# Layer 0 of a two-layer model on one core: the second batch's attention placed within the Sinkhorn chain, branch sums on GpSimd, and the mix taken from PSUM copies in two halves

## The chip, the core and the metric

The kernel runs on one core of a Trainium2 chip. The core has a matrix engine (TensorE, in profiles PE; its weight loads are PEld), a vector engine (VectorE, DVE), an activation engine (ScalarE, ACT), a general engine (GpSimd, POOL) and a queue engine (SyncE, SP) that issues DMAs. Each works through its own instructions in order and waits on semaphores for the others. SBUF is the working memory, PSUM the memory that matmuls write to; GpSimd does not use PSUM here.

The metric is the device time of one execution, in microseconds (us). Several runs are made, and their median is given. A profile is one further execution, with its own time and its own span.

## The reference

Two batches of 1024 rows, 512 wide, go through two layers. Layer 0, cut to what matters here:

```python
xn = _layernorm(x)
x = x + _L0_attn_ref(xn, ...) + _L0_ffn_ref(xn, ...)
# attention: one head of 128
out = softmax(q @ k.T * scale) @ v ;  out @ Wo + bo
# ffn: four streams of 128 columns
H_res = sinkhorn_log((x_norm @ W_res.T).reshape(B, T, 4, 4) + H_res_base)   # 50 iterations
H_pre, H_post = softmax(x_norm @ W_pre.T + ...), softmax(x_norm @ W_post.T + ...)
H_res = (1 - g) * I + g * H_res
y = einsum('btnc,btn->btc', x_streams, H_pre) @ W_branch
x_mixed = einsum('btij,btjc->btic', H_res, x_streams)
return x_mixed + einsum('btc,btn->btnc', y, H_post)
...
def step(carry, _):
    u = -logsumexp(Z + v[..., None, :], axis=-1)
    v = -logsumexp(Z + u[..., :, None], axis=-2)
```

Layer 1 has causal attention with 32 heads in 8 groups over low-rank keys and values, and beside it a linear layer with routed low-rank parts. It needs the normed output of layer 0, first through its "latents", a projection of all 1024 rows of a batch.

## The kernel before

Rows lie in tiles of 128, eight to a batch; `acc[b, t]` is the running sum of tile t of batch b, an SBUF tile of 128 x 512. Matmuls take float16 pairs (a high and a low part, three products), so most data is split: ACT writes the high part, DVE or POOL subtracts it for the low part. `normed_T` normalises a tile, splits it and has SP transpose it by DMA. Its `pool` argument says which engines do that.

The kernel is written against a framework that schedules when the program is complete: an instruction earlier in the program has the higher priority, a simulated timeline decides when its inputs and buffers are there, and the result is a fixed order on every engine. Buffers come from pools by tag ("P" three, "PT" three, "xr" four, "f2k" four, "wo" five, "wq" four, "h2k" three; in PSUM "s" four, "pp" three, "av" one). `tc.issue_after(i)`, and `after(...)` around it, put the instructions of a block behind instruction i on its engine.

The order of layer 0 in the program (lines 897 to 948):

- `front0(0)`: norm, transposes, values and ffn logits, Q and K of batch 0.
- `sinkhorn(0)` is a generator. It begins on line 471, and its iterations for batch 0 are in `chain_dve` (line 542), in linear form: `Kt`, the exponentials of the 4 x 4 matrices of 1024 rows (128 x 128 numbers), lies in PSUM; each iteration multiplies, sums and takes the reciprocal over rows (lines 551 to 553), then over columns (556 to 558), all on DVE, each instruction needing the one before. The column sum reads `M` with its last two axes exchanged. At iteration 25 the sums are taken back into the logarithms (560 to 564). There are 100 yields; `adv(n)` moves the chain by n of them. At the end lines 508 and 510 write `Hm`, from which the mix is computed.
- Batch 0's attention in two halves of four row blocks. A row block is a `row_step`: scores on PE, two evictions with a row minimum on DVE (`rows_exp`, L272), exponential on ACT (L276), scaling into the high part (L295, or L292 and L293), the low part on DVE (L301) or, where `LP[b]` names the block, on POOL (L299), and a DMA transpose (L303). `attn0_out` then multiplies by the values (L328), projects (L465, L467) and adds to `acc` on DVE (L469). Between these calls the chain is advanced by `CA = 5` steps per row block.
- `branch0(0)`: y = the branch, scaled on ACT (L420), summed on POOL. `CB = 1` step per tile.
- `front0(1)` and `branch0(1)`, with `CC = 2` steps at each of 16 places and `CB` at eight.
- `adv(200)`: the rest of the chain. `hm0` is its last instruction.
- The weights of layer 1's first group (`load_q`, `kv0`) on POOL's queue.
- Two groups of four tiles (`LG`): `mix0_units`, then `layernorm_tiles`, then `xT_tile` for each. A unit loads x again and norms it on ACT (L579), then works five streams: four of x, the fifth of y. For the tiles in `MP` ACT multiplies into a tile `m` (L592) and POOL adds it to `acc` (L593); for the others DVE does 4 fused multiply-adds a stream (L602), the first from `acc` into a PSUM tile `d`, the last back into `acc`.
- `layer1_attn` calls `start`: the latents of batch 0 from the first four tiles, four q units, the latents of the other four, keys and values of group 0, and then `attn0_1()`: batch 1's attention of layer 0, whose row blocks stand behind `hm0`.

After that come 16 groups of layer 1 (eight heads groups for each batch) with 32 row blocks each. Further work is put at numbered steps by `put`: the chain of batch 1 (on POOL), its mix, `branch0_add(1, t)` (the branch's product and addition, lines 434 and 436), gating, and the ffn blocks; those of batch 1 at every second step from the start of the last group.

Of the kernel before, what the change touches and what calls it, by code (L numbers as in the profile page):

```python
# [16 lines left out]
P = 128  # L17
# [13 lines left out]
NR = P // QR  # L31
LG = ((0, 1, 2, 3), (4, 5, 6, 7))
MP = (1, 3, 6, 7)
NP = (2, 2, 2, 2, 0, 2, 0, 2)
LP = ((0, 1, 2, 4, 5, 6, 7), (0,))
F0 = (((0, 1, 2, 3), (4, 5, 6, 7)), (range(0, 8),))
FP = ((0, 2, 0, 2, 0, 2, 0, 2), (2, 2, 2, 2, 2, 2, 2, 2))
X1 = 7
CA, CB, CC = 5, 1, 2
SK0, SKN, MX0, MXN, LN1 = 1, 116, 122, 74, 198  # L40

G0, G1, GL, WT, LX, LA = 16, 200, 3, 220, 231, 240
# [9 lines left out]
def tile_model(ctx: ExitStack, tc: tile.TileContext, out: bass.AP, a: dict):  # L52
# [126 lines left out]


    last_pool, last_row, last_T = [None], [None], [None]
    last_hi, last_lo, last_hm = [None], [None], [None]

    def after(*insts):

# [21 lines left out]
    def layernorm_tiles(b, mv, rs, ts):  # L207
        ve = T("ve", [P, NT], bufs=2)
        sl = slice(ts[0], ts[-1] + 1)
        for t in ts:  # L210
            st = T("bnst", [P, 6], bufs=2)
            V.bn_stats(st, acc[b, t])
            V.bn_aggr(mv[:, t, :], st)
        V.tensor_scalar(ve[:, sl], mv[:, sl, 1], LN_EPS, None, ALU.add)
        rsqrt(rs[:, 0, sl], ve[:, sl], "rs")
        V.tensor_scalar(rs[:, 2, sl], rs[:, 0, sl], 4.0, None, ALU.mult)
        V.scalar_tensor_tensor(rs[:, 1, sl], mv[:, sl, 0], -1.0, rs[:, 2, sl],
                               ALU.mult, ALU.mult)

    def normed_T(b, mv, rs, t, dst, pool, tags=(("f2k", FB), ("h2k", HB))):  # L220

        xn = T(tags[0][0], [P, NC, P], bufs=tags[0][1])
        xf = xn.rearrange("p c d -> p (c d)")
        hl = T(tags[1][0], [P, NC, 2, P], F16, bufs=tags[1][1])
        if pool == 2:
            A.activation(xf, acc[b, t], AF.Identity, scale=rs[:, 2, t:t + 1], bias=rs[:, 1, t:t + 1])
        elif pool:
            G.tensor_scalar(xf, acc[b, t], rs[:, 2, t:t + 1], rs[:, 1, t:t + 1], ALU.mult, ALU.add)
        else:
            V.tensor_scalar(xf, acc[b, t], rs[:, 2, t:t + 1], rs[:, 1, t:t + 1], ALU.mult, ALU.add)  # L230
        last_hi[0] = A.activation(hl[:, :, 0, :], xn, AF.Copy)
        eng = G if pool else V
        lo = eng.tensor_tensor(hl[:, :, 1, :], xn, hl[:, :, 0, :], ALU.subtract)
        (last_pool if pool else last_lo)[0] = lo
        last_T[0] = nc.sync.dma_start_transpose(dst, hl.rearrange("p c l d -> p (c l d)"))

    def proj_T(w, xT, half):
# [7 lines left out]
    def srow():  # L245
        count[0] += 1
        return ps.tile([P, 512], F32, tag="s", name=f"s_{count[0]}", bufs=BS)
# [223 lines left out]
    def sinkhorn(b, lg):  # L471
# [33 lines left out]

        chain = chain_dve if b == 0 else chain_pool
        yield from chain(b, Z, M, aa, bb, over_i, over_j, f2)
        V.tensor_scalar(Hb, M, gs[:, 0:1], None, ALU.mult)
        for n in range(4):
            last_hm[0] = V.tensor_scalar(Hb[:, :, n, n], Hb[:, :, n, n], gs[:, 1:2], None, ALU.add)  # L510

    def chain_pool(b, Z, M, aa, bb, over_i, over_j, f2):

# [27 lines left out]

    def chain_dve(b, Z, M, aa, bb, over_i, over_j, f2):

        cols = M.rearrange("p t i j -> p t j i")
        Kt = srow()[:, :NT * 16].rearrange("p (t i j) -> p t i j", i=4, j=4)
        A.activation(Kt, Z, AF.Exp)
        x = Kt
        yield
        for it in range(1, 50):
            if x is not Kt:  # L550
                V.tensor_tensor(M, Kt, over_i(bb), ALU.mult)
            V.tensor_reduce(aa, x, AX.X, ALU.add)
            V.reciprocal(aa, aa)
            x = M
            yield
            V.tensor_tensor(f2(M), f2(Kt), over_j(aa), ALU.mult)  # L556
            V.tensor_reduce(bb, cols, AX.X, ALU.add)
            V.reciprocal(bb, bb)
            if it == 25:
                A.activation(aa, aa, AF.Ln)  # L560
                A.activation(bb, bb, AF.Ln)
                V.tensor_tensor(f2(Z), f2(Z), over_j(aa), ALU.add)
                V.tensor_tensor(Z, Z, over_i(bb), ALU.add)
                A.activation(Kt, Z, AF.Exp)
                x = Kt
            yield
        V.tensor_tensor(M, M, over_i(bb), ALU.mult)

    def mix0_units(b, t, rs, pool, y=None, hh=None):


        got = {}

        def load():
            xr = got["xr"] = T("xr", [P, H], bufs=XB)
            with after(t0):
                nc.sync.dma_start(xr, a["x"][(b * NT + t) * P:(b * NT + t + 1) * P, :])
            if b == 0:
                A.activation(xr, xr, AF.Identity, scale=rs[:, 2, t:t + 1], bias=rs[:, 1, t:t + 1])  # L579
                return  # L580
            with tc.issue_after(p0.ins):
                G.tensor_scalar(xr, xr, rs[:, 2, t:t + 1], rs[:, 1, t:t + 1], ALU.mult, ALU.add)

        n = NC if y is None else NC + 1

        def stream(j):
            xj = y if j == NC else got["xr"][:, j * P:(j + 1) * P]
            by = [hh[:, t, 1, i:i + 1] if j == NC else Hm[b][:, t, i, j:j + 1] for i in range(NC)]
            if pool:
                m = T("f2k", [P, H], bufs=FB)  # L590
                for i in range(NC):
# [1 line left out]
                G.tensor_tensor(acc[b, t], acc[b, t], m, ALU.add)  # L593
                return

            if j == 0:
                got["d"] = PP()
            for i in range(NC):
                sl = slice(i * P, (i + 1) * P)
                src = acc[b, t] if j == 0 else got["d"]  # L600
                dst = acc[b, t] if j == n - 1 else got["d"]
                V.scalar_tensor_tensor(dst[:, sl], xj, by[i], src[:, sl], ALU.mult, ALU.add)  # L602

        return [load] + [lambda j=j: stream(j) for j in range(n)]

# [302 lines left out]
    attn0_out(0, 0, f0[0][2], PTs)  # L910
    PTs = attn0_rows(0, 1, *f0[0][:2], lambda: adv(CA))
    attn0_out(0, 1, f0[0][2], PTs)
    f0[1] = front0(1, lambda: adv(CC))
    y4s = branch0(1, *f0[1][3:5], lambda: adv(CB))
    adv(200)
    hm0 = last_hm[0]

    def attn0_1():
        for half in range(2):
            with after(hm0):  # L920
                PT = attn0_rows(1, half, *f0[1][:2])
            attn0_out(1, half, f0[1][2], PT)

    def new_xT(b):
        xT1[b] = T("xT", [P, NT, 2 * NC, P], F16, bufs=1)

    def xT_tile(b, t, pool):
        normed_T(b, *ln1[b], t, xT1[b][:, t], pool)

    def tile_of(b, t):  # L930
        d = T("h2k", [P, 2 * NC, P], F16, bufs=HB)
        normed_T(b, *ln1[b], t, d, True, (("f2k", FB), ("xr", XB)))
        return d

    for hh in range(4):
        load_q(0, hh)
    kv0 = kv(0, 0)
    kv0[1][0]()
    new_xT(0)
    ln1[0] = layernorm(0, "b")  # L940
    for k, ts in enumerate(LG):
        units = [mix0_units(0, t, f0[0][5], t in MP, ys0[t], f0[0][4]) for t in ts]
        for fs in itertools.zip_longest(*units):
            for f in fs:
                f()
        layernorm_tiles(0, *ln1[0], ts)
        for t in ts:
            xT_tile(0, t, NP[t])

    def start(kvf, q):  # L950
        latents(0)
# [5 lines left out]
            lat_evac(0, mc, 1, lat_block(0, wl[:, mc], 1))  # L957
        for f in kvf:
            f()
        attn0_1()  # L960

    gw1 = gating_w()
    chain = sinkhorn(1, logit[1])
# [58 lines left out]
    put(58, 2, ffn_w)  # L1022
    for t in range(NT):
        put(0, FF + t, lambda t=t: ffn_block(0, t))
        put(60, 2 * t, lambda t=t: ffn_block(1, t))
    layer1_attn(kv0, start, extra)


# [45 lines left out]
```

## Time and profile before

| what | value |
|---|---|
| median of 3 runs | 1951.74 us (1942.79 to 1952.55) |
| the profiled execution's own time | 1957.52 us |
| its span | 1955.7 us, 35314 instructions |
| busy, PE / DVE / ACT / POOL | 1746.8 / 1506.1 / 1201.5 / 885.5 us |
| chain's first exponential (L546) | 48.19 us |
| `Hm` complete (L592 begins) | 183.03 us |
| first matmul of the latents | 235.3 us |
| first score of layer 1 (128 x 32) | 279.1 us |
| PE busy in 1100 to 1900 us | 98 to 100 of each 100 us |

The span is the time between the first and last event of the profile; the execution's time is a little longer. A row of the windows names a stretch and gives for each engine the busy microseconds and the number of instructions. A group's row names line, engine, operation, the tile written and the tiles read, the shape, and how many there were. A wait's row says which instruction waited for which, and for how long in total. Idle time of an engine that is not on the path costs nothing.

### The profile page before, as it was taken

The numbers are of one execution on the slowest core, as the hardware profiler recorded it, in microseconds if no ns is written. First come the engines' busy times: TensorE is split into PE (matmuls) and PEld (weight loads), VectorE is DVE, ScalarE is ACT, GpSimd is POOL, SyncE is SP. The second block draws the span as 40 slices with busy tenths as digits, with TensorE's granted clock in tenths as the row PEclk, the third lists the DMA queues.
The fourth block names the chain that finished last, engine by engine and source line by source line (L and its number), as shares of the span: only waits on it lengthen the run. The fifth ranks groups of instructions, "written<-read, shape, count | busy, mean of one in ns | idle before, by whom it ended". The sixth has DMA issues, their size and how long they took to land. (4 is left out here: it accounts for less than half of the span.)

```text
span 1955.7 us, 35314 instructions
## 1 busy us (share of the span) xinstructions
PE 1746.8 (89%) x11458; PEld 1051.5 (54%) x11458; DVE 1506.1 (77%) x4065; ACT 1201.5 (61%) x2924; POOL 885.5 (45%) x1527
## 2 busy tenths in 40 slices
PE   4771499989998999989889899999999999999997
PEld 3340245555564555555554556666566666656654
DVE  8889768988786878787875676777778787878665
ACT  4752864566665777776544565767666666666554
POOL 5553429676766655444631636060515152436010
PEclk9885699999999999999989999999999999999999
DMA  6430524565654656465753864655555565657446
GB/s 200 87 65 10 126 58 98 126 126 113 124 120 95 136 112 143 107 127 117 156 120 52 166 131 119 130 122 133 123 129 128 128 131 119 134 117 156 94 93 138
DMA packets 707308, 230.27 MB, mean 118 GB/s; under 512 B 689953, under 2 KB 690081, under 8 KB 707122
## 3 DMA queue, kind: packets, MB, share of 16 engines
q1 hardware_dynamic: 691666, 180.75, 45.7%
q0 software_dynamic: 13152, 43.07, 8.4%
q10 hardware_dynamic: 2304, 4.20, 0.7%
q8 instruction: 90, 1.47, 0.3%
q14 instruction: 96, 0.79, 0.1%
HBM read 52.81 MB, written 4.19 MB: 29 GB/s over the span
## 5 line engine op out<-in xcount | busy, mean ns | idle before, releaser
L301 DVE SCALAR_TENSOR_TENSOR Phl<-P,r,Phl 128x1024 f16<-128x1024 f32 (+31 forms) x520 | 483.2, 935 | 179.3 <-ACT Phl L295 168.5
L276 ACT ACTIVATE P<-P,nm 128x1024 f32<-128x1024 f32 (+31 forms) x528 | 391.9, 742 | 315.7 <-DVE nm L268 301.2
L88 PE MATMUL s<-K,Q 128*128 128x512 f16 (+22 forms) x2400 | 450.7, 320 | 88.9 <-DVE sk L556 38.2
L328 PE MATMUL av<-PT,V 128*128 128x256 f16 x3648 | 458.8, 277 | 27.8 <-DMA PT<-Phl 18.2
L295 ACT ACTIVATE Phl<-P,r 128x1024 f16<-128x1024 f32 (+31 forms) x520 | 379.8, 737 | 115.2 <-DMA PT<-Phl 95.0
L328 PEld LDWEIGHTS <-V 128*128 128x128 f16 x3648 | 360.0, 99 | 127.8 <-DMA PT<-Phl 22.2
L88 PE MATMUL pp<-wo,ao 128*128 128x512 f16 x1536 | 373.8, 380 | 18.1 <-ACT ao L103 17.0
L285 POOL MEMSET Phl<- 128x192 f16 (+2 forms) x384 | 77.3, 204 | 655.9 <-DMA PT<-Phl 525.4
L88 PE MATMUL pp<-xT,wq 128*128 128x512 f16 x1536 | 374.0, 384 | 0.0
L88 PEld LDWEIGHTS <-Q 128*128 128x128 f16 x2400 | 225.2, 99 | 247.0 <-issue 104.9
L88 PEld LDWEIGHTS <-wq 128*128 128x128 f16 x1536 | 150.9, 99 | 169.2 <-issue 9.0
L88 PEld LDWEIGHTS <-ao 128*128 128x128 f16 x1536 | 147.8, 98 | 172.7 <-ACT ao L103 23.3
L268 DVE CUSTOM_DVE_ANT_0 P<-s,mask,nm 128x272 f32<-128x272 f32 (+15 forms) x256 | 156.9, 615 | 7.0 <-PE s L88 0.7
L94 POOL TENSOR_SCALAR f2k<-f2k 128x512 f32<-128x512 f32 x164 | 115.0, 702 | 89.9 <-DMA f2k<-in_Wq 50.6
L272 DVE TENSOR_SCALAR_CACHE_REDUCE P<-s 128x512 f32<-128x512 f32 (+15 forms) x272 | 152.4, 563 | 2.0 <-PE s L88 1.0
L289 DVE RECIPROCAL r<-r 128x1 f32<-128x1 f32 x528 | 80.5, 157 | 82.8 <-ACT P L276 78.3
L290 ACT ACTIVATE r<-r 128x1 f32<-128x1 f32 x528 | 96.0, 193 | 71.3 <-DVE r L289 69.5
L268 DVE CUSTOM_DVE_ANT_0 P<-s,mask 128x32 f32<-128x32 f32 (+15 forms) x256 | 106.9, 432 | 16.1 <-PE s L88 13.3
L104 DVE SCALAR_TENSOR_TENSOR Q<-pp,Q 128x512 f16<-128x512 f32 x128 | 87.3, 682 | 26.5 <-ACT Q L103 26.4
L103 ACT ACTIVATE ao<-av 128x512 f16<-128x512 f32 x128 | 74.6, 583 | 53.7 <-PE av L328 48.3
L104 DVE SCALAR_TENSOR_TENSOR ao<-av,ao 128x512 f16<-128x512 f32 x128 | 87.6, 684 | 22.2 <-ACT ao L103 21.7
L103 ACT ACTIVATE Q<-pp 128x512 f16<-128x512 f32 x128 | 74.2, 580 | 49.2 <-PE pp L88 48.7
(251 smaller groups left out, 2106.1 us busy)
## 6 DMA issues: line engine op xcount, KB each, us to landing
f2k<-in_Wq POOLq DMA_DIRECT2D x64, 256.0 KB, 3.4
f2k<-in_WoT POOLq DMA_DIRECT2D x64, 256.0 KB, 3.7
PT<-Phl SPq DMA_TRANSPOSE x528, 3.4
acc<-in_x SPq DMA_DIRECT2D x16, 256.0 KB, 5.0
xr<-in_x SPq DMA_DIRECT2D x16, 256.0 KB, 3.5
f2k<-in_Wup POOLq DMA_DIRECT2D x16, 256.0 KB, 3.3
out<-acc ACTq DMA_DIRECT2D x16, 256.0 KB, 3.4
f2k<-in_Wlat POOLq DMA_DIRECT2D x8, 256.0 KB, 6.1
```

Source lines behind the costliest of these rows:

```text
L88: nc.tensor.matmul(dst, lhs(l), rhs(r), start=(i == 0 and j == 0), stop=(i == n - 1 and j == 2))
L94: G.tensor_scalar(stage, stage, scale, 1.0, ALU.mult, ALU.mult)
L103: A.activation(hl_hi, src, AF.Copy, scale=scale)
L104: return V.scalar_tensor_tensor(hl_lo, src, scale, hl_hi, ALU.mult, ALU.subtract)
L268: last_row[0] = V.tensor_tensor_reduce(Pm[:, o:o + w], pt[:, :w], mask[:, 512 - w:], -scale, first, ALU.add, ALU.min, nm[:, k:k + 1])
L272: last_row[0] = V.tensor_scalar(Pm[:, o:o + w], pt[:, :w], -scale, first, ALU.mult, ALU.min, accum_out=nm[:, k:k + 1])
L276: A.activation(Pm[:, :W], Pm[:, :W], AF.Exp, bias=last, scale=-1.0, accum_out=r[:, 0:1])
L289: V.reciprocal(r[:, 1:2], r[:, 0:1])
L290: A.activation(r[:, 1:2], r[:, 1:2], AF.Copy, scale=PSCALE)
L295: A.activation(hl[:, 0, :W], Pm[:, :W], AF.Copy, scale=r[:, 1:2])
L301: V.scalar_tensor_tensor(hl[:, 1, :W], Pm[:, :W], r[:, 1:2], hl[:, 0, :W], ALU.mult, ALU.subtract)
L328: nc.tensor.matmul(p, Vh(j, l), PT(r * nj + j), start=(j == 0 and k == 0), stop=(j == nj - 1 and k == 2))
```

## The change

The constants: `LP[1]` goes from one to six row blocks with the low part on POOL; `CA, CB, CC` become 4, 1, 1 and a new `CD = 3`; `NP`, the engines for the tiles' norm, becomes `(3, 0, 3, 0, 0, 2, 0, 2)`, where 3 means norm on ACT and low part on DVE.

The chain holds the matrix a second time, exchanged, in the same PSUM bank. Then the column step writes and sums `M` in order:

```diff
-            V.tensor_tensor(f2(M), f2(Kt), over_j(aa), ALU.mult)
-            V.tensor_reduce(bb, cols, AX.X, ALU.add)
+            V.tensor_tensor(M, KT, over_i(aa), ALU.mult)
+            V.tensor_reduce(bb, M, AX.X, ALU.add)
...
+        def kernels():
+            A.activation(Kt, Z, AF.Exp)
+            A.activation(KT, Kt.rearrange("p t i j -> p t j i"), AF.Copy)
```

Batch 1's attention moves from `start` to a place ahead of the rest of the chain, which is advanced by `CD` steps a row block; the weights' loads move with it, and the branch of batch 0 is added by POOL ahead of `front0(1)`:

```diff
+    for t in range(NT):
+        branch0_add(0, t, ys0[t], f0[0][4])
     f0[1] = front0(1, lambda: adv(CC))
     y4s = branch0(1, *f0[1][3:5], lambda: adv(CB))
+    kv0 = kv(0, 0)
+    for half in range(2):
+        if half:
+            kv0[1][0]()
+        for hh in (2 * half, 2 * half + 1):
+            load_q(0, hh)
+        PTs = attn0_rows(1, half, *f0[1][:2], lambda: adv(CD))
+        attn0_out(1, half, f0[1][2], PTs)
     adv(200)
...
-        attn0_1()
```

The mix loses its fifth stream. For DVE's tiles `load` also copies `acc` to PSUM on ACT, so that the first stream reads PSUM; tiles 4 to 7 of x go into halves of two "P" buffers:

```diff
+            if b == 0 and t >= 4:
+                if t % 2 == 0:
+                    xr_more[t] = T("P", [P, 2, H], bufs=PB)
+                xr = got["xr"] = xr_more[t & ~1][:, t % 2]
...
+                if not pool:
+                    got["d"] = srow() if t < 4 else PP()
+                    A.activation(got["d"], acc[b, t], AF.Copy)
...
+            if b == 0 and (not pool or j > 1):
+                with after(*(last_rs[:1] if pool else last_rs[1:] if j else last_mix)):
+                    stream_at(j)
```

`last_mix` is the first half's last multiply-add, `last_rs` the first half's last high part (ACT) and the last instruction of its norm (DVE); for the first half all three are empty. So in the second half DVE's first stream comes behind the first half's mix, its others behind the first half's norm, and ACT's streams 2 and 3 behind the first half's transposed tiles. The tiles' norm for batch 0 uses other buffers:

```diff
-        normed_T(b, *ln1[b], t, xT1[b][:, t], pool)
+        normed_T(b, *ln1[b], t, xT1[b][:, t], pool, (("f2k", FB), ("h2k", HB)) if b else
+                 (("xr", XB), (("h2k", HB), ("wo", WB))[t % 2]))
```

Last, the ffn blocks of batch 1 are spread over the last group:

```diff
-        put(60, 2 * t, lambda t=t: ffn_block(1, t))
+        put(60, 4 * t + 3, lambda t=t: ffn_block(1, t))
```

## The prediction

> **What bounds the kernel now.** I read the page's busy tenths first, then windows cut at the places where the work changes, then the waits of the stretch in which TensorE (PE) stands still, then the timeline there. The tenths say where to look: PE is at 9 almost everywhere after slice 5, and slice 4 (147 to 196 us) holds a 1.
>
> ```profile
> PE   4771499989998999989889899999999999999997
> DVE  8889768988786878787875676777778787878665
> ```
>
> The windows (length, then busy us and instructions of PE, weight loads, DVE, ACT, POOL, then clock, DMA share, GB/s) give layer 0's second half by stage.
>
> ```profile
> 48.00:66.00 18.00, 12.12 (x104) 7.18 (x103) 17.06 (x66) 17.37 (x51) 9.96 (x15) 0.91 0.00 1
> 66.00:88.00 22.00, 15.08 (x78) 7.99 (x77) 19.92 (x67) 18.61 (x28) 13.13 (x10) 0.81 0.74 134
> 144.00:182.30 38.30, 0.76 (x2) 0.25 (x2) 34.64 (x107) 1.00 (x4) 13.32 (x19) 0.50 0.03 7
> 182.30:235.00 52.70, 20.41 (x86) 9.99 (x84) 47.23 (x150) 43.83 (x108) 25.20 (x21) 0.66 0.46 100
> 235.00:262.00 27.00, 23.98 (x108) 11.07 (x109) 18.09 (x38) 20.20 (x49) 13.55 (x15) 0.90 0.43 78
> ```
>
> From 144 to 182 only the Sinkhorn chain runs; from 182 to 235 DVE and ACT carry mix 0 and batch 1's attention together, and PE is 20 of 53. The waits of 131 to 290 (total, times, longest) name both holes: the scores held behind the chain, and the latents waiting for transposed tiles.
>
> ```profile
> PE s L88 <- DVE sk L556: 38.2, 1, 38.2
> ...
> PE pp L88 <- DMA xT<-h2k: 7.9, 1, 7.9
> ```
>
> One iteration of the chain, alone on DVE, and the next one's start:
>
> ```profile
> 178.01 0.29 DVE L551 TENSOR_TENSOR sk<-s,sk 128x128 f32<-128x128 f32 x1
> 178.33 0.29 DVE L552 TENSOR_REDUCE sk<-sk 128x32 f32<-128x128 f32 x1
> 178.65 0.35 DVE L553 RECIPROCAL sk<-sk 128x32 f32<-128x32 f32 x1
> 179.04 0.29 DVE L556 TENSOR_TENSOR sk<-s,sk 128x128 f32<-128x128 f32 x1
> 179.37 0.37 DVE L557 TENSOR_REDUCE sk<-sk 128x32 f32<-128x128 f32 x1
> 179.78 0.35 DVE L558 RECIPROCAL sk<-sk 128x32 f32<-128x32 f32 x1
> 180.16 0.29 DVE L551 TENSOR_TENSOR sk<-s,sk 128x128 f32<-128x128 f32 x1
> ```
>
> The period is 2.15 us of which 1.94 is DVE: there is hardly room between two steps. So until layer 1's first score (279.1 us) the path is chain, mix, norm, transposes, latents; after it PE is the bound.
>
> **Term 1, the chain's end (Hm at 183.0 us): later by 21.** Batch 1's attention now shares DVE with the chain. Its DVE rows, from 182 to 262 and after: 16 score evictions (L272) 12.9 us with their accumulator reads, 8 reciprocals 1.3, two low parts (L301) at 1.28 = 2.6 instead of seven, 8 output adds (L469) 5.5: 22.3 us. What such work costs the chain I take from batch 0's, which already runs inside it: in the first two windows above the chain did 6 and 6.5 iterations, 27.0 us alone, in 40.0; it lost 13.0 for 12.7 us of other DVE work (37.0 less 12.5 x 1.94). So a microsecond costs one: +22.3. Stalls of DVE in its own order: batch 0 had 6.6 us on these instructions between 48 and 144 (L469 5.9); I take half, +3. The second copy of the matrix makes the column sum contiguous: L557 0.377 us becomes L552's 0.285, 49 times, -4.5; two more ACT copies of 128 x 128 at 0.27 (L564), +0.5. The steps handed out ahead of the flush are 91 of 100 in both orders (3+20+8+20+32+8 before, 3+16+8+16+16+8+24 after): nothing. Sum +21. Bounds: +10 if the 0.21 us gaps of 49 iterations (10 us) swallow that much, +30 with all of the stalls and a late front.
>
> Hidden in this term: eight branch sums on POOL, which has the rows already for batch 1,
>
> ```profile
> L434 POOL TENSOR_TENSOR f2k<-ysum,hh x8: 1029/1032/1273, 300.3 to 334.8; 128x512 f32<-128x512 f32 x8
> ...
> L436 POOL TENSOR_TENSOR acc<-acc,f2k x8: 1254/1264/1283, 304.6 to 339.9; 128x512 f32<-128x512 f32 x8
> ```
>
> 8 x 2.30 = 18.4 us, against 28 idle of 56 on POOL between 88 and 144. They are ahead of front0(1)'s eight low parts (L233, 1.16) in its queue; at worst the second four (9.2 us) delay Q and K of batch 1, while the chain goes on. Six low parts (L299, 2.13) and the loads of Wq and Wup, which keep their queue and place behind branch0(1) (2.4 each with the splits), fall where POOL was 13 of 38. The uncovered price is the front's 9 us. ACT gets 5 more passes of 1.1 us (pool rows take two) and four copies of acc to PSUM, 0.62 to 0.80 (L231, L226), between 135 and 200 where it was nearly idle. SP gets the eight transposes of PT and tiles 4 to 7 of x; the latter wait for P buffers, free when the last row is transposed.
>
> The Trainium skill, GPSIMD Engine Reference, section 4.1, speaks against the sums: elementwise work belongs on VectorE, GpSimd being about 2x slower on two inputs. The rows say 2.30 us on POOL against 4 x 0.35 on DVE; by the rule the move would lose 0.9 us a tile if POOL were on the path.
>
> **Term 2, Hm to the first latent matmul: 52.3 us (183.0 to 235.3) becomes 25, -27.** Alone, the first half is: ACT's products for tiles 1 and 3, 32 at 0.30 (twenty in 5.95), 9.5; POOL's eight adds (1.27) trail to 11.4; DVE's 32 for tiles 0 and 2 take 8.5 (nine in 2.40). Two tiles' statistics behind that, 1.7; the small norm chain 3.5 (247.3 to 251.1); tiles to transpose, ACT 2 x 0.80 + 4 x 0.62, 4.1, with their low parts on DVE (0.69) now; last transpose issued to PE start 3.2 (232.16 to 235.33) and hand-overs 1: 25. Before, rows of the attention and the fifth stream sat between these. Bounds 22 and 33 (the second half's first ACT products and low parts in between). The order by hand keeps the second half behind the norm; its own end, about 17 us later, is early enough, since the first latents and four q units occupied PE 29 us (235.3 to 264.4).
>
> Within this lies the source of the products:
>
> ```profile
> L602 DVE SCALAR_TENSOR_TENSOR pp<-xr,Hm,pp x48: 333/351/365, 193.0 to 224.7; 128x128 f32<-128x128 f32 x48
> L602 DVE SCALAR_TENSOR_TENSOR pp<-xr,Hm,acc x16: 331/352/1414, 184.1 to 206.3; 128x128 f32<-128x128 f32 x16
> ```
>
> With acc in SBUF an instruction took up to 1.41 us while POOL added; from a PSUM copy never above 0.37. The Trainium skill, SBUF — State Buffer, Who interferes with whom, says why: a DVE instruction with two SBUF inputs and a GpSimd one that reads SBUF block each other. It also speaks against the change: with POOL busier, L562, L567 and two L301 in the chain may each wait for a 2.1 us POOL pass, 8 us by the rule; L562 took 1.22 us here beside a POOL pass, its twin L563 0.29.
>
> **Term 3, first latent to first score: 43.8 us becomes 38, -6.** 48 matmuls of batch 1's AV (24 in 2.79 us) leave this stretch; bounds -10 and 0 (the second half's mix beside the latents' evictions).
>
> **Term 4, behind 279 us: -8.** Batch 1's output projection, 40 matmuls of 512 columns at 0.22 (48 of L88's in 10.52), 8.8 us, ran between 286 and 303 on a PE with hardly a gap. Bounds -9 and 0, if DVE or POOL set that pace.
>
> **Term 5, the tail: -2.** ffn blocks of batch 1 move from every second step to 4t+3; the last, 12 short and 15 long matmuls (about 3.9 us), now follows the last scores, where PE stood 4.85 us before the last AV. Bounds -4, and +3 if its transpose gets in front of the last PT.
>
> Sum: +21 - 27 - 6 - 8 - 2 = -22. The profiled execution took 1957.52 us (span 1955.7); the median shown is 1951.74, 0.3% below. So 1935.5 for such an execution, 1929.7 for the median: **1930**.
>
> **Rivals.**
> - Forecast, 0.55: own range 1917 to 1943.
> - The chain hides the attention in its gaps and stalls, 0.2: term 1 is +8 (12.5 of work beyond the gaps less 4.5) and the rest stands: -35, 1917. For it: chain-alone DVE still idles 10%. Against it: the one-for-one price in the first windows.
> - Layer 1's first group gives half back, 0.13: its steps carry chain 1, mix 1 and gating at fixed places, and DVE was 48 of 50 between 350 and 400. Then term 4 is 0, and of the 12 us won up to the first score 6 stay: -6 - 2 = -8, 1944. Against it: PE was 46 to 48 of 50 from 250 to 500.
> - Slower, 0.12: DVE, which works in order, moves the chain only by the three steps handed out per row. If front0(1) slips by 9 and the rows go at batch 0's pace (first score 47.6, last add 108.9: 61 us for eight), the last add falls at 144 + 9 + 61 = 214 with nine half steps of 1.1 us left: Hm at 224, +41; the last low parts then stand before mix 0's adds on POOL, and term 2 ends at 33: 41 - 19 - 6 - 8 - 2 = +6, 1958. It decides from Hm at 218. Against it: in 66 to 88 DVE was busy 19.9 of 22 under such rows, and the chain did 6.5 iterations.
>
> No edit can be void: the 38 us wait has its one cause in L920, which goes.
>
> **Chances.** A measurement of this kernel tells about 0.5% (10 us) from no change: faster needs 1942 or less. The forecast gives faster 0.53 of its 0.55, the hidden chain all 0.2, the give-back 0.05 (0.08 no change), the forecast's rest 0.02 and the slow case 0.04 no change and 0.08 slower. Faster 0.78, same 0.14, slower 0.08. Range 1909 (the hidden chain with term 2 at 22 and term 3 at -10, rounded up) to 1952, which leaves out most of the slow case.
>
> **What would show it.** Hm near 204 us with rows of batch 1 before it; PE no longer idle after 144; first latent about 25 us later; first 128x32 score near 267; L557's reduce at 0.29; no L469 after it; the last ffn behind the last score. Hm beyond 215, or POOL waits in front of front0(1)'s transposes, would make it wrong.

## The result and the profile after

The changed kernel took 1923.57 us (median of 4 runs, 1917.84 to 1926.57) against 1950.8 us for the kernel before beside it: ratio 0.9865, 95% interval 0.9826 to 0.9903, so 27 us or 1.35% less. The forecast was 1930. The profiled execution has a span of 1924.8 us against 1955.7. One execution of e_ffn below took 2237.57 us at a granted clock of 0.795, a slower state of the core, and is left out of its median and ratio.

The tenths row of PE (TensorE) and DVE of the changed kernel, to be set beside the one shown of before:

```profile
PE   4766399999999989999899899999999999999998
...
DVE  8888967987887868686965767777778787878675
```

Slice 4 (147 to 196 us by the old cut, 144 to 192 by the new) held a 1 and now holds a 6: the scores and products of batch 1 run where PE stood still. Slice 5 holds a 3, where before it had a 4: this is the mix, which is still there.

The windows from 144 us on, with cuts at the end of the kernel before's hole (182.3), at the chain's end (198.4), the first latent matmul (228.3) and layer 1's first score (268.2). Columns: length, then busy us and instructions of PE, weight loads, DVE, ACT, POOL, then clock, DMA share, GB/s.

```profile
144.00:182.30 38.30, 25.92 (x178) 14.41 (x176) 33.37 (x114) 33.77 (x72) 28.57 (x32) 0.84 0.46 99
182.30:198.40 16.10, 12.56 (x69) 7.43 (x70) 13.57 (x35) 5.42 (x8) 10.57 (x15) 0.75 0.67 173
198.40:228.30 29.90, 2.03 (x9) 0.50 (x7) 29.05 (x95) 23.82 (x74) 21.15 (x18) 0.59 0.21 41
228.30:268.20 39.90, 35.83 (x151) 15.36 (x152) 24.45 (x55) 18.14 (x44) 32.68 (x39) 0.92 0.33 77
```

Between 144 and 182 PE goes from 0.8 to 25.9 us busy and ACT from 1.0 to 33.8, with DVE where it was (34.6, now 33.4). Between the chain's end and the first latent PE is busy 2 us of 30 and DVE 29 of 30: DVE is the engine that is full in this hole now. The waits of PE from 131 to 290 (total, times, longest) say the same; the 38 us wait of the scores on the chain is gone, and one on the transposed tiles has grown from 7.9 to 26.9 us:

```profile
PE pp L88 <- DMA xT<-h2k: 26.9, 1, 26.9
PE av L328 <- DMA PT<-Phl: 4.8, 3, 3.1
...
PE pp L88 <- DVE cmp L104: 3.4, 1, 3.4
```

Where the time came from, by five points of the trace (us; "+" is the distance from the point before; the last column is the distance from layer 1's first output add on DVE to the end of the span):

| kernel | chain's end Hm | first latent | layer 1's first score | its first output add | rest |
|---|---|---|---|---|---|
| before | 183.0 | 235.3 (+52.3) | 279.1 (+43.8) | 321.9 (+42.7) | 1633.8 |
| changed | 198.4 | 228.3 (+29.9) | 268.2 (+39.9) | 296.7 (+28.5) | 1628.1 |
| changed, second profile | 196.0 | 225.9 (+29.8) | 264.0 (+38.1) | 293.5 (+29.5) | 1627.8 |

The second profile is of the same program, taken beside the experiments of section 8. It differs by 2 to 4 us at these points: a difference of that size between two profiles tells nothing. Where it matters, both profiles are given below.

### The profile page after: what moved, and what is told of

It reads as the page before. It is cut to its first block, busy times and chain, and to the rows that moved or that the text cites. A ratio compares the mean times of both kernels' runs of the same rounds, so it can differ in the third digit from the quotient of the medians.

```text
span 1924.8 us, 35319 instructions
## 1 busy us (share of the span) xinstructions
PE 1743.7 (91%) x11458; PEld 1050.0 (55%) x11458; DVE 1487.2 (77%) x4050; ACT 1204.1 (63%) x2917; POOL 902.4 (47%) x1540
## 5 line engine op out<-in xcount | busy, mean ns | idle before, releaser
L301 DVE SCALAR_TENSOR_TENSOR Phl<-P,r,Phl 128x1024 f16<-128x1024 f32 (+31 forms) x515 | 469.8, 917 | 180.1 <-ACT Phl L295 168.4
L295 ACT ACTIVATE Phl<-P,r 128x1024 f16<-128x1024 f32 (+31 forms) x515 | 374.1, 733 | 109.1 <-DMA PT<-Phl 92.1
L328 PEld LDWEIGHTS <-V 128*128 128x128 f16 x3648 | 359.4, 99 | 121.8 <-DMA PT<-Phl 16.1
L268 DVE CUSTOM_DVE_ANT_0 P<-s,mask 128x32 f32<-128x32 f32 (+15 forms) x256 | 106.3, 430 | 13.2 <-PE s L88 10.6
L88 PEld LDWEIGHTS <-xT 128*128 128x128 f16 x864 | 65.1, 104 | 80.1 <-DMA xT<-h2k 43.5
L88 PE MATMUL pp<-cmp,xT 128*128 128x128 f16 (+2 forms) x720 | 88.1, 277 | 20.5 <-DMA xT<-h2k 15.8
L104 DVE SCALAR_TENSOR_TENSOR Q<-pp,Q 128x512 f16<-128x512 f32 x128 | 87.1, 681 | 25.3 <-ACT Q L103 25.2
```

Source lines behind the costliest of these rows:

```text
L88: nc.tensor.matmul(dst, lhs(l), rhs(r), start=(i == 0 and j == 0), stop=(i == n - 1 and j == 2))
L104: return V.scalar_tensor_tensor(hl_lo, src, scale, hl_hi, ALU.mult, ALU.subtract)
L268: last_row[0] = V.tensor_tensor_reduce(Pm[:, o:o + w], pt[:, :w], mask[:, 512 - w:], -scale, first, ALU.add, ALU.min, nm[:, k:k + 1])
L295: A.activation(hl[:, 0, :W], Pm[:, :W], AF.Copy, scale=r[:, 1:2])
L301: V.scalar_tensor_tensor(hl[:, 1, :W], Pm[:, :W], r[:, 1:2], hl[:, 0, :W], ALU.mult, ALU.subtract)
L328: nc.tensor.matmul(p, Vh(j, l), PT(r * nj + j), start=(j == 0 and k == 0), stop=(j == nj - 1 and k == 2))
```

## The experiments

All ratios are to the kernel before, measured beside the kernel in question, with a 95% interval.

**1. Batch 1's layer-0 attention left out (e_none).** Its scores, softmax, AV products and output projection are not computed; everything else of the change stays.

```diff
-        PTs = attn0_rows(1, half, *f0[1][:2], lambda: adv(CD))
-        attn0_out(1, half, f0[1][2], PTs)
```

> The changed kernel with batch 1's attention of layer 0 left out (its row blocks and its output projection; all else as changed). It measures what that attention costs the Sinkhorn chain. Theory (DVE is the chain's bound, a microsecond of other DVE work costs it about one): Hm, at 198.4 us with the change, comes 19 us earlier, at 179 (176 to 182); the first score of layer 1, at 268.2, moves with it to 249 (246 to 253), and nothing behind it moves, since PE did that attention under the chain: 1905 us. Rival (the chain's gaps hold the attention, and its end is set elsewhere): Hm not before 193, time within 6 us of 1923.6.

Chain's end at 181.8, 16.6 us earlier than in the changed kernel (14.3 than in its second profile); first latent +28.1, first score 250.0; 1899.5 us, 5 less than expected, ratio 0.973 (0.9692 to 0.9768). The windows from the first reduce of the chain to Hm (columns as above), of the kernel before, of this run and of the changed kernel:

```profile
39.82:183.03 143.21, 79.64 (x561) 46.56 (x559) 124.22 (x411) 69.54 (x161) 63.24 (x73) 0.77 0.29 63
39.84:181.78 141.94, 77.42 (x550) 47.73 (x547) 120.25 (x411) 75.51 (x171) 81.37 (x92) 0.79 0.32 71
39.70:198.37 158.67, 111.80 (x731) 64.84 (x729) 136.26 (x457) 101.86 (x211) 96.88 (x100) 0.82 0.41 88
```

From this run to the changed kernel DVE is busy 16.0 us longer and idle 0.7 longer (21.7, then 22.4; in the second profile 15.1 longer busy and 0.4 less idle). So the attention is not hidden in the chain's gaps: it costs 14 to 17 us there, all of it as work of DVE. From the kernel before to this run, which has the second matrix and the rest of the change, DVE has 4.0 us less work and 2.7 more idle time, and the chain's end is only 1.3 us earlier.

**2. The placement alone (b_place).** The kernel before, with batch 1's attention inside the chain, the hand-out counts and the low parts of the change; no sums on GpSimd, no second matrix, the mix as before, the feed-forward blocks as before.

```diff
-CA, CB, CC = 5, 1, 2
+CA, CB, CC, CD = 4, 1, 1, 3
-LP = ((0, 1, 2, 4, 5, 6, 7), (0,))
+LP = ((0, 1, 2, 4, 5, 6, 7), (0, 1, 2, 4, 5, 6))
...
+        PTs = attn0_rows(1, half, *f0[1][:2], lambda: adv(CD))
+        attn0_out(1, half, f0[1][2], PTs)
     adv(200)
-        attn0_1()
```

> The kernel before with the placement alone: batch 1's attention and the weight loads ahead of the rest of the chain, LP[1] and CA, CB, CC, CD as changed; one matrix, the fifth stream, the mix from acc and the ffn blocks stay. Theory (placement is the larger part): Hm at 202 (198 to 206), first latent 35 to 42 us behind it instead of 52.3, first score near 280, and behind it the 14 us that the output projection took: span 1937 to 1945, 11 to 19 us under 1955.7, ratio 0.990 to 0.994. Rival (the rework of the mix makes the gain, the placement only moves the chain's end): first score at 290 or later, ratio 0.997 or more.

Chain's end 201.6, first latent +35.1, first score 274.7, first output add 307.9 (before 321.9). 1943.75 us, ratio 0.9937 (0.9909 to 0.9966): the placement alone is a gain of 0.6%. The profiled span, 1931.4, is below the expected range; that execution was the fastest of the ten. From the chain's end to the first score it takes 73.1 us, the kernel before 96.1, the changed one 69.8 (68.0 in its second profile): 23.0 of the 26 to 28 us that this stretch gives come from moving the attention out of it. The 3 to 5 that are left, for the mix's rework, are hardly more than two profiles differ by.

**3. The feed-forward blocks at every second step again (e_ffn), and the other way round, at 4t+3 in the kernel before (b_ffn).**

```diff
-        put(60, 4 * t + 3, lambda t=t: ffn_block(1, t))
+        put(60, 2 * t, lambda t=t: ffn_block(1, t))
```

> The changed kernel with the ffn blocks of batch 1 put back at every second step of the last group. The trace of the change gives the last group 6 us (its lead over before grows from 25.1 to 31.4). Theory (the blocks at the end fill PE's wait for the last PT, 6.5 us before, 0.9 after): the span is 5 to 7 us longer than 1924.8, the wait of AV for PT in the last group is back at 5 to 7. Rival (the size of the prediction, 2 us, the rest being chance of that execution): 1 to 3 us, the wait 3 or less.

> The kernel before with one line of the change: batch 1's feed-forward blocks of layer 1 at steps 4t+3. By the runs so far (the last block fills TensorE's wait before the last AV products, where the kernel before waited 6.5 us and the changed one 2.1) it ends 4 to 9 us earlier than before, ratio 0.995 to 0.998, and the last group of layer 1 shows it. By the prediction's own term -2, ratio 0.999. Rival, it wins nothing alone because the blocks displace work earlier in layer 1: ratio 1.000 or above.

e_ffn: 1928.8 us (three runs, 1925.6 to 1933.4), ratio 0.9877 (0.9833 to 0.9921), which the intervals do not tell from the changed kernel's 0.9865. Its profiled span, 1923.8, is not the 5 to 7 us above 1924.8 that were expected: what the end loses, layer 1 has gained before. b_ffn: 1945.5 us, ratio 0.9962 (0.9938 to 0.9986): alone the new steps take 0.38% off, 7 to 8 us. The trace has it in the last group of layer 1. PE's waits for the last transposed probabilities there (total, times, longest), first in the kernel before, then in b_ffn, then in e_ffn:

```profile
PE av L328 <- DMA PT<-Phl: 6.5, 4, 4.8
```

```profile
PE av L328 <- DMA PT<-Phl: 0.4, 1, 0.4
```

```profile
PE av L328 <- DMA PT<-Phl: 8.4, 5, 5.0
```

In the changed kernel it is 0.9. Between the 113th and the 128th of layer 1's output adds pass 187.1 us before and 180.8 in b_ffn; 180.9 changed (182.3 in the second profile) and 189.7 in e_ffn. So the tail is worth 5 to 9 us, not the 2 of term 5: the 12 short and 15 long matmuls of one block were set against one wait of 4.85, but with blocks at every fourth step 0.4 to 0.9 us is left of all four waits together.

**4. One matrix in the chain (e_single).** The transposed copy is left away, and the column sums read M in strides, as before.

```diff
-            V.tensor_tensor(M, KT, over_i(aa), ALU.mult)
-            V.tensor_reduce(bb, M, AX.X, ALU.add)
+            V.tensor_tensor(f2(M), f2(Kt), over_j(aa), ALU.mult)
+            V.tensor_reduce(bb, cols, AX.X, ALU.add)
```

> The changed kernel with one matrix in the chain, the column sum strided again. Theory: the reduce takes 0.377 us instead of 0.284, 49 times: Hm 4.0 to 4.6 us later than 198.4, the first score as much later than 268.2, the time 4 us longer. Rival (the chain's end is set by the attention's rows beside it, not by its own instructions): Hm moves by less than 1.5 us and so does the time.

Chain's end 195.2: not later, but 3.2 us earlier than in the changed kernel's first profile and 0.8 earlier than in its second; 1921.35 us, ratio 0.9841 (0.9798 to 0.9884). The 4.0 to 4.6 us of the theory did not come; the rival, less than 1.5 us, fits the second profile. DVE's groups from 48 to 200 us (busy, mean ns of one | idle before them and what ended it), first of the changed kernel, then with one matrix:

```profile
L563 DVE TENSOR_REDUCE sk<-sk 128x32 f32<-128x128 f32 x49 | 13.9, 284 | 1.3
...
L272 DVE TENSOR_SCALAR_CACHE_REDUCE P<-s 128x512 f32<-128x512 f32 x16 | 10.8, 676 | 3.8 <-PE s L88 2.0 <-POOL Phl L299 1.8
L469 DVE SCALAR_TENSOR_TENSOR acc<-pp,acc 128x512 f32<-128x512 f32 x14 | 9.1, 674 | 1.9 <-PE pp L467 1.9
L301 DVE SCALAR_TENSOR_TENSOR Phl<-P,r,Phl 128x1024 f16<-128x1024 f32 x3 | 4.3, 1426 | 2.6 <-ACT Phl L295 2.6
```

```profile
L561 DVE TENSOR_REDUCE sk<-sk 128x32 f32<-128x128 f32 x49 | 18.4, 375 | 1.1
...
L272 DVE TENSOR_SCALAR_CACHE_REDUCE P<-s 128x512 f32<-128x512 f32 x16 | 10.9, 680 | 1.6 <-PE s L88 0.9 <-POOL Phl L299 0.7
L469 DVE SCALAR_TENSOR_TENSOR acc<-pp,acc 128x512 f32<-128x512 f32 x15 | 9.9, 680 | 1.2 <-PE pp L467 1.2
L301 DVE SCALAR_TENSOR_TENSOR Phl<-P,r,Phl 128x1024 f16<-128x1024 f32 x3 | 4.0, 1322 | 2.3 <-ACT Phl L295 2.3
```

The reduce does cost 91 ns more each, 4.5 us in all. But DVE's waits for PE, GpSimd and ACT in the attention's rows are shorter: 8.3 us of idle in front of these three groups become 5.1. The window from the chain's first reduce to Hm, here:

```profile
38.99:195.20 156.21, 108.94 (x720) 63.29 (x718) 138.16 (x458) 101.28 (x208) 95.64 (x99) 0.81 0.42 93
```

DVE is idle 18.1 us in it, against 22.4 and 21.3 in the two profiles of the changed kernel, and busy 138.2, against 136.3 and 135.3: 2 to 3 us more work stand against 3 to 4 us less idle time. One reading is that the steps of the attention come when the other engines deliver, and chain steps that end sooner wait there; experiment 1 fits it, since without the attention, too, DVE's idle time had grown by 2.7 us. No run isolates it. The saving on the rows is real, and none of it is seen at the chain's end.

**5. The sums of batch 0 back in the mix (e_branch).** No sums on GpSimd; y is the fifth stream of the mix again.

```diff
-    for t in range(NT):
-        branch0_add(0, t, ys0[t], f0[0][4])
...
-        units = [mix0_units(0, t, f0[0][5], t in MP) for t in ts]
+        units = [mix0_units(0, t, f0[0][5], t in MP, ys0[t], f0[0][4]) for t in ts]
```

> The changed kernel with batch 0's branch sums as before: no sums on GpSimd, y comes back as a fifth stream of the mix. By the theory of the front (the eight sums, 18.4 us on GpSimd, held batch 1's low parts, Q and K back by about 9 us, and the chain ran on meanwhile): batch 1's Q and K come some 9 us earlier, but the chain's end (198.4 us in the changed kernel) moves by less than 3; the mix is longer by eight DVE products of 0.35, 16 ACT products of 0.30 with GpSimd's adds behind them, so chain's end to first latent is 32 to 34 instead of 29.9, and the kernel ends 0 to 5 us later. Rival, the late front delays the chain's end one for one: the chain's end comes at 189 to 192 and the kernel ends 3 to 7 us earlier, 1918 or below.

Chain's end 200.0, first latent +29.7, first score 271.1; 1921.0 us, ratio 0.9853 (0.982 to 0.9885). PE's wait for batch 1's transposed tiles in the front, 100 to 200 us, first in the changed kernel, then here:

```profile
PE pp L88 <- DMA xT<-h2k: 15.8, 5, 12.5
```

```profile
PE pp L88 <- DMA xT<-h2k: 3.9, 3, 2.1
```

The sums do hold the front up (the 48 matmuls on batch 1's tiles start at 131.1 against 118.9), and the chain's end does not come earlier without them: the delay is covered, as the prediction had it. The rival falls. The end is a little later even (200.0 against 198.4 and 196.0): with the front earlier, all 16 output adds of layer 0's attention on DVE fall ahead of Hm, in the changed kernel 12. The same holds of every run with this attention inside the chain: with 12 of them Hm comes at 194.7 to 198.4, with 16 (b_place, e_branch, e_lp0, c_lean) at 200.0 to 206.6. The first part of the theory stands, its price in the mix was not seen: 29.7, not 32 to 34. The first score comes 2.9 and 7.1 us later than in the two profiles of the changed kernel.

**6. Without the order by hand (e_order).** DVE may take products of the second half ahead of the first half's norm.

```diff
-            if b == 0 and (not pool or j > 1):
-                with after(*(last_rs[:1] if pool else last_rs[1:] if j else last_mix)):
-                    stream_at(j)
-            else:
-                stream_at(j)
+            stream_at(j)
```

> The changed kernel without the order by hand that keeps the second half's products behind the norm of the first half. Theory: DVE and ACT take second-half products ahead of the first half's norm, so chain's end to first latent grows from 29.9 to 34 to 42 us (up to the 12 us that a half's products take), and the kernel ends 3 to 10 us later than the changed one. Rival, the compiler's own order is the same or the order only costs: 29.9 stays within 2 and the time too.

First latent +38.6 instead of 29.9, inside the theory's range. DVE's timeline there (start, duration, line, operation):

```profile
204.16 0.60 DVE L616 SCALAR_TENSOR_TENSOR pp<-P,Hm,pp 128x128 f32<-128x128 f32 x2
204.67 0.60 DVE L616 SCALAR_TENSOR_TENSOR s<-xr,Hm,s 128x128 f32<-128x128 f32 x2
205.19 0.60 DVE L616 SCALAR_TENSOR_TENSOR pp<-P,Hm,pp 128x128 f32<-128x128 f32 x2
...
217.90 2.25 DVE L214 TENSOR_SCALAR ve<-mvb 128x4 f32<-128x4 f32 x1
...
222.49 0.46 DVE L198 TENSOR_SCALAR rs<-rs 128x4 f32<-128x4 f32 x1
```

Products of the two halves alternate, and the norm's small steps (L214 to L198) stand between further products, the first at 217.9 where the changed kernel has it at 214.4. But then first latent to first score takes 35.8 instead of 39.9 (38.1 in the second profile), and the first score comes at 271.5. The second half's mix ends on DVE at 222.6 instead of 227.3, and PE's later wait for `cmp`, 3.4 us in the changed kernel, is gone. 1928.8 us (1917.5 to 1930.2), ratio 0.9879 (0.9837 to 0.9922): against the changed kernel no difference that this resolves.

**7. The first stream from the accumulator in SBUF (e_acc).** The four copies to PSUM go.

```diff
-                    A.activation(got["d"], acc[b, t], AF.Copy)
...
+ ... xj, by[i], (acc[b, t] if j == 0 else got["d"])[:, sl], ALU.mult, ALU.add)
```

> The changed kernel, but the first stream of the mix reads the accumulator in SBUF; the four ACT copies to PSUM are gone. Theory: the first half's eight first products on DVE stand beside GpSimd's adds and some take up to 1.41 us instead of 0.35, +1 to +4 us from chain's end to first latent (29.9). Rival, the copies cost as much as they save, because ACT carries the products of two tiles meanwhile: within 1 us, or earlier by the 0.6 to 0.8 of a copy.

First latent +34.6, 4.7 us later, a little over the theory's range. The first half's products on DVE (lowest/median/highest ns) with their accumulator from SBUF here, and from the PSUM copy in the changed kernel:

```profile
L619 DVE SCALAR_TENSOR_TENSOR s<-xr,Hm,acc x8: 349/1356/1391, 197.1 to 205.2; 128x128 f32<-128x128 f32 x8
```

```profile
L620 DVE SCALAR_TENSOR_TENSOR s<-xr,Hm,s x24: 345/347/350, 198.9 to 207.2; 128x128 f32<-128x128 f32 x24
```

While GpSimd adds, five of the eight take 1.36 us and one 0.76, against 0.35: 5.5 us more on DVE, of which the path took 4.7. The first score, 268.7, is 0.5 us later than in the first profile of the changed kernel and 4.7 later than in the second; the time, 1924.4 us, ratio 0.9875 (0.9838 to 0.9911), does not show it. The Trainium skill, SBUF — State Buffer, Who interferes with whom, names the cause, a DVE instruction with two SBUF inputs beside a GpSimd one that reads SBUF; the rows agree, at nearly four times the duration.

**8. The changed kernel again, and three more beside it on one chip.** Again (a_again):

> The changed kernel once more, beside the next three on one chip: chain's end 196 to 199, first latent 29.5 to 30.2 behind it, first score 266 to 269, ratio to before 0.983 to 0.990. What it differs by from its first profile is what one execution differs from another.

1923.1 us, ratio 0.9836 (0.9801 to 0.987); points in the table above. First score 264.0, 2 us under the expected range.

Only one of batch 1's eight low parts on GpSimd (e_lp0):

```diff
-LP = ((0, 1, 2, 4, 5, 6, 7), (0, 1, 2, 4, 5, 6))
+LP = ((0, 1, 2, 4, 5, 6, 7), (0,))
```

> The changed kernel with only one of batch 1's eight low parts of P on GpSimd, as in the kernel before; five more passes of 1.3 us, 6.5 us in all, stand on DVE within the chain. If DVE's work has the price seen when the attention was left out (0.74 us each us), the chain's end comes 4.8 us later, 201 to 204. If it goes as with the second matrix (4.9 us of DVE work moved nothing, DVE's waits grew instead), the chain's end stays at 196 to 200. By the prediction's one for one: 203 to 206.

```profile
L301 DVE SCALAR_TENSOR_TENSOR Phl<-P,r,Phl 128x1024 f16<-128x1024 f32 x8 | 10.4, 1301 | 2.8 <-ACT Phl L295 2.8
```

Chain's end 206.6, just above the range of one for one: eight low parts of both batches before Hm instead of three (10.4 us against 4.3), with four output adds that fell behind Hm before (2.5). By the windows from the chain's first reduce to Hm, DVE is busy 142.9 us against 136.3 and 135.3, 6.6 and 7.6 more, and idle 24.6 against 22.4 and 21.3; Hm comes 8.2 and 10.6 us later. This work of DVE is paid in full; the second matrix was the exception. Yet the kernel takes 1920.5 us, ratio 0.9831 (0.9792 to 0.987), no longer than the changed one. It is 7.4 us behind the first changed profile at layer 1's first output add, and 3.4 ahead at the 65th.

One matrix and all eight low parts on GpSimd (c_single8), an attempt at a better kernel:

> The changed kernel with one matrix in the chain as before, and all eight low parts of batch 1 on GpSimd, which takes 2.6 us more off DVE. If what runs beside the chain sets its end: chain's end 192 to 196, first score 259 to 264, ratio 0.981 to 0.986, 0 to 6 us ahead of the changed kernel. Rival, GpSimd's passes of 2.1 us become the wait: chain's end 198 or later.

Chain's end 194.7, first score 262.2, both as expected; 1921.3 us, ratio 0.9829 (0.9796 to 0.9862), 1.8 us below the changed kernel on the same chip. That is no difference these runs resolve. No version was found that beats the changed kernel for certain.

Three parts undone at once, one matrix, y in the mix, no PSUM copies (c_lean; the diffs are those of 4, 5 and 7):

> The changed kernel with three of its parts undone at once: one matrix in the chain, y as a fifth stream of the mix, no PSUM copies of the accumulator. What is left is the attention inside the chain, the low parts on GpSimd, the order by halves and the feed-forward blocks' steps. If each of the three is hidden by itself: first score 265 to 272, and the time within 5 us of the changed kernel's on this chip (ratio 0.983 to 0.991). Rival, each was hidden only because the others stood: first score 276 or later and 6 us or more behind the changed kernel.

Chain's end 202.8, first latent +33.3, first score 276.5; 1930.7 us, ratio 0.9889 (0.9851 to 0.9926), 7.6 us over the changed kernel on that chip. The rival has it by both its numbers: none of the six runs (1926.9 to 1936.7) is as fast as the slowest of the changed kernel's six (1925.3). None of the three showed a price in the time alone. Whether they stood in for each other, as the rival has it, or are small prices that add up is not settled: at layer 1's first output add, experiments 4, 5 and 7 lie -2.6, +9.0 and +4.4 us from the changed kernel's second profile, +10.8 together, and c_lean +12.0; from the first profile it is -5.8, +5.8 and +1.2, and c_lean +8.8.

**Layer 1.** From its first output add to the 65th the kernels take different times for the same work: 886.8 us before, 882.5 and 883.0 changed, 871.7 in e_lp0, 872.3 in e_branch, 874.5 in b_place, 884.6 in c_lean. In e_lp0 the order of PE's instructions there is nearly that of the changed kernel: around one place some AV products and projections change places. Part of the difference goes with the granted clock. By windows over this stretch PE is busy 813.2 us in b_place and e_order at a clock of 0.99, 815.7 in e_lp0 at 0.98, and 821.2 and 821.8 in the kernel before and the changed one at 0.97; over all fourteen profiles PE is busy the longer the lower the clock (correlation -0.94). PE's idle time there, 54 to 66 us, does not go with the clock. From the 65th add to the 113th it is 552.6 to 563.5. So e_lp0's 7.4 us at layer 1's door were gone 870 us later. Whether an early entry causes such a loss is not settled: e_none had its first score 18.1 us earlier and ended 24 us earlier.

## Why the prediction came out

The forecast was -22 on the profiled execution; its profile gave -30.9 and the median -27. By its own terms:

- **Term 1, chain's end +21: measured +15.3 (13.0 in the second profile).** Right in kind, too large. With e_none as the step between, the attention is +16.6 (14.3) instead of 22.3 + 3, and the rest of the change -1.3 instead of -4. The step that failed is the price by rows. Of the 22.3 us, 19.4 stand ahead of Hm: 11.5 of score evictions, 2.4 of reciprocals and accumulator reads, 3.0 of low parts, 2.5 of output adds; the other four adds (2.7) fell behind Hm, which ends the chain and not the attention, so the sign "no L469 after it" did not come. And rows overlap their neighbours on DVE a little, so that its busy time grew by 16.0 and not by 19.4. DVE's idle time did grow by about the +3 (19.0 to 22.4 us), but 2.7 of it is there without the attention (experiment 1): it took back most of the matrix's -4.5, which shows on the reduce's rows (18.4 to 13.9 us) and, by experiment 4, not at the chain's end. The Trainium skill's price against it (SBUF — State Buffer, Who interferes with whom, 8 us by its rule) came to about 2: L508 took 1.27 us instead of 0.29, L568 0.95 instead of 0.29, and one low part (L301) 1.71 instead of 1.28, once each; the kernel before had one such case, L562 with 1.22.
- **Term 2, chain's end to first latent -27: measured -22.3.** 29.9 instead of 25, inside the bounds of 22 and 33. The timeline (start, duration, engine, line, operation) shows each step:

```profile
198.37 4.78 ACT L613 ACTIVATE f2k<-xr,Hm 128x128 f32<-128x128 f32 x16 [1.46 <-DVE Hm L508]
...
199.38 1.28 DVE L469 SCALAR_TENSOR_TENSOR acc<-pp,acc 128x512 f32<-128x512 f32 x2
...
201.94 0.68 DVE L469 SCALAR_TENSOR_TENSOR acc<-pp,acc 128x512 f32<-128x512 f32 x1
...
207.45 2.15 DVE L620 SCALAR_TENSOR_TENSOR acc<-xr,Hm,s 128x128 f32<-128x128 f32 x8
...
209.52 0.60 DVE L620 SCALAR_TENSOR_TENSOR pp<-P,Hm,pp 128x128 f32<-128x128 f32 x2
210.03 1.28 DVE L212 BATCH_NORM_STATS2 bnst<-acc 128x6 f32<-128x512 f32 x2
...
212.38 1.28 DVE L212 BATCH_NORM_STATS2 bnst<-acc 128x6 f32<-128x512 f32 x2
213.57 0.60 DVE L620 SCALAR_TENSOR_TENSOR pp<-P,Hm,pp 128x128 f32<-128x128 f32 x2
...
214.36 0.94 DVE L214 TENSOR_SCALAR ve<-mvb 128x4 f32<-128x4 f32 x1
...
216.80 0.16 DVE L217 SCALAR_TENSOR_TENSOR rsb<-mvb,rsb 128x4 f32<-128x4 f32 x1
...
220.46 1.29 DVE L233 TENSOR_TENSOR wo<-xr,wo 128x512 f16<-128x512 f32 x2
...
222.18 1.54 DVE L233 TENSOR_TENSOR h2k<-xr,h2k 128x512 f16<-128x512 f32 x1
...
224.13 1.27 SPq L235 DMA_TRANSPOSE xT<-h2k  x1
...
228.32 1.01 PE L88 MATMUL pp<-xT,PT 128*128 128x512 f16 x2 [26.86 <-DMA xT<-h2k]
```

The first half ends at 209.5, 11.2 after Hm (forecast 11.4), although four output adds of the attention (199.4 to 202.6) sit in it. The statistics were taken as two tiles behind the mix, 1.7 us; they end at 214.4, 4.8 us on: all four tiles' stand there (2.8 us), and eight products of the second half (pp<-P,Hm,pp, 2.0 us) alternate with them. The norm takes 2.6 (forecast 3.5). Tiles to the last low part take 6.8 (forecast 4.1): more second-half products, and a low part of 1.54 us instead of 0.69. From there 4.6 to PE (forecast 4.2). So the stretch is 4.9 longer than worked out, and the step that failed is "two tiles' statistics behind that" and "4.1", and with them "the order by hand keeps the second half behind the norm": by the change's own conditions DVE's first stream of the second half waits for the first half's mix alone, and the others come between the tiles of the norm. Without the attention in the way (e_none) the stretch is 28.1.
- **Term 3, first latent to first score -6: measured -3.9 (-5.7).** Inside its bounds. In experiment 6 it moves against term 2: what delayed the first latent to the second half's good came back here in part. In experiment 7, against the second profile, it does not (38.1 in both).
- **Term 4, behind the first score -8: measured -14.2 (-13.2) to the first output add.** The step that failed is the list: it has the projection's matmuls and nothing else. The windows from first score to first output add, before, then changed, and one tile of the projection before (two matmuls of L465 and three of L467, then the next work):

```profile
279.14:321.85 42.71, 40.67 (x246) 20.31 (x246) 37.16 (x98) 26.99 (x83) 33.53 (x53) 0.96 0.44 85
268.18:296.67 28.49, 27.85 (x212) 16.93 (x212) 22.90 (x78) 20.89 (x70) 19.75 (x36) 1.00 0.32 74
```

```profile
292.88 0.60 PE L465 MATMUL pp<-wo,row 1*128 1x512 f16 x2
293.41 0.82 PE L467 MATMUL pp<-wo,wo 128*128 128x512 f16 x3
294.07 0.61 PE L88 MATMUL s<-K,Q 128*128 128x352 f16 x3
```

Five matmuls in 1.19 us here, from start to start; all 40 took 10.3 us, 0.26 each and not 0.22, so the price itself was short by 1.5. With them went ten AV products of 28 (1.7 us), four scores of 48 (2.0) and 1.4 us of PE's idle time, and 20 more of another group's small matmuls came in (1.1): 14.2 together. The granted clock has a part in it: the window 288.2 to 291.6 of the kernel before has 0.50, the changed kernel 1.00 throughout. At half the clock 3.4 us hold 1.7 us of work, so about 1.7 of the 14.2 is this by estimate; whether the change removed that spell no run shows. No half was given back at once: the rival of the first group's give-back fails at its place.
- **Behind that, taken as nothing:** 25.2 us of lead at the first output add is 25.2 at the 113th, with swings of 19 to 34 between. In the kernels of experiment 8 such swings end differently by up to 10 us. This is the part of the forecast that has no basis yet.
- **Term 5, the tail -2: measured -6.2 between the 113th and the last output add** (-4.8 in the second profile), the same in b_ffn (-6.3); e_ffn loses 8.8. Mis-sized, as said at experiment 3: one wait of 4.85 was counted, and all waits for PT there were 6.5.

Terms 2 and 3 fell short by 6.7, terms 1, 4 and 5 went beyond by 16.1: five sizes off in two directions, and a sum 9.4 us off (8.9 on the span). That 1930 lies within 6.4 us of the result is in part luck: the misses cancel in part, and the stretch of layer 1 whose times differ by 15 us between kernels happened to keep the lead. By time, the placement alone gives 0.63% and the new steps of the feed-forward blocks alone 0.38%, both clear of no change: if they add, 1.0 of the 1.35%. What is left for the rework of the mix and of the chain no run isolates.

The rival of the hidden chain (1917) is as near in time as the forecast (6.6 us below the result, the forecast 6.4 above), and its price for the attention, 12.5, is nearer to the measured 14.3 to 16.6 than the forecast's 25.3. But its mechanism is not what happened: the gaps swallowed nothing, DVE's idle time is 21.7 us without the attention and 22.4 and 21.3 with it. The slower case decided from Hm at 218; the latest Hm of all runs was 206.6.

The sums on GpSimd cost the path nothing that was seen (experiment 5). The Trainium skill, GPSIMD Engine Reference, section 4.1, would have them on VectorE for their duration; here POOL's time was not on the path.

## What to carry to other kernels

A dependent chain that holds an engine at 90% is a place to put independent work, but the work is paid for nearly in full on that engine; the gain is what the other engines do meanwhile, so count what moves out of the stage behind. Take busy time from a window's union and not from a sum of rows, which overlap, and space matmuls from start to start. Price a moved block by everything that moves with it and by all the waits that it can fill, not by the nearest one. Undo parts together as well as one by one: prices too small to be seen singly can show in their sum.

## What the runs showed of the hardware

A DVE product of 128 x 128 with both inputs in SBUF takes 1.36 us (five of eight) beside GpSimd's adds, and 0.35 with one input in PSUM. A reduce of 128 x 32 from a strided 128 x 128 takes 0.375 us, contiguous 0.284. Nearly the same instructions of layer 1 took 872 to 887 us over one stretch from kernel to kernel. PE's busy time in it, 813 to 822 us, goes with the granted clock, 0.99 to 0.97; its idle time there, 54 to 66 us, does not. What sets the one or the other was not found.
